# A two-layer graph convolution: layer 2's first chunks gather rows before they are normalised

## The chip, the cores and the metric

The kernel runs on one core of a Trainium2 chip. The metric is the device time of one execution in microseconds (us). The kernel before takes 2332.54 us, the median of three runs (2331.6 to 2333.5). The engines are called by their names in the profile: PE is TensorE (PEld its weight loads), DVE is VectorE, ACT is ScalarE, POOL is GpSimd, SP is SyncE, which here only issues transfers.

## What is computed

A graph of N = 6250 nodes (128 features) and E = 106250 edges, sorted by destination, goes through two attention layers with two heads of 64 columns. Between them every feature is normalised over all nodes and passed through a ReLU. The result is added to the input and each row is normalised.

```python
def conv(h, edge_attr, src, dst, Wq, bq, Wk, bk, Wv, bv, We, Ws, bs):
    q, k, v = (heads(h @ W + b) for W, b in ((Wq, bq), (Wk, bk), (Wv, bv)))
    e = heads(edge_attr @ We)
    alpha = einsum('ehc,ehc->eh', q[dst], k[src] + e) / sqrt(C)
    a = softmax of alpha over the edges of one dst
    return segment_sum((v[src] + e) * a[:, :, None], dst) + h @ Ws + bs
...
edge_attr = concatenate([cos((last_update[src] - t)[:, None] * time_w + time_b), msg])
h = conv(x, edge_attr, ...)
mu = h.mean(axis=0)
var = ((h - mu) ** 2).mean(axis=0)
h = relu((h - mu) / sqrt(var + 1e-05) * bn_g + bn_b)
out = layernorm(x + conv(h, edge_attr, ...))
```

Layer 2 needs mu and var over all nodes, so nothing of its scores can be computed before layer 1 has ended. The product k[src] is not formed: q is multiplied with the weights of k ahead of time and stored per destination node (the "tables"), so that a chunk's scores are products of raw source rows with a table.

## The kernel before

A plan at the start cuts the sorted edges into NC = 107 chunks of consecutive destination nodes, each of at most 1024 edges (T = 8 tiles of 128) and at most NN = 64 nodes. It computes the first node of each chunk (nbs) and its first edge (sls). If the plan's limits hold, `ordered` runs; otherwise `general`, which is another program for the same result.

`ordered` runs `conv(0, ...)` and `conv(1, ...)`, one loop over the chunks each, written out by hand in program order (`manual_schedule`). For chunk k:

- `fetch(k)` (L714): SP loads the edge attributes into the tile ff, the chunk's part of the table (ftab), and in layer 2 the stored time encoding (fz), the stored transposed edge attributes (into fxT, which serves as their buffer) and the residual rows (fr).
- `gather(k)` (L740): eight indirect transfers issued by GpSimd, each of 128 source rows, from xv_d in layer 1 and from h_d in layer 2.
- `turn_in` (L783): TensorE transposes the gathered rows (fpx), ScalarE copies them out of PSUM (fft). Layer 1 also transposes the edge attributes.
- `score` (L803), `lowest`, `weigh`: scores in PSUM (fps), their minimum per row on VectorE, the exponential on ScalarE (fs).
- `turn_weights` (L824), `gather_sums` (L835): weights transposed (fpt), then eight products accumulate the sums of a chunk in fpa.
- `divide`, `finish_turn`, `finish` (L841 to L897): division, multiplication with Wv and We. Layer 1 stores the chunk's columns into hT (features on partitions, nodes along the free axis), layer 2 adds the residual and collects groups of chunks (STARTS) for the row norm.

In a round k of the loop the chunks k+4 (fetch, gather), k+1 (turn_in), k (score), k-1 (sums) and k-2 (finish) are in work. Layer 1's time encoding is a sine on ScalarE, one chunk at a time for the first rounds (up to SINGLE = 24), then in pairs; the sine and the exponential are in different function tables.

The tables of a layer are made in blocks of 512 nodes (`tables`, L622): layer 1 has five products of 128x512 a block, layer 2 four, each evacuated with a bias, and the block stored with one transfer issued by ScalarE. `residual` makes res_d, x + h @ Ws + bs, in layer 2. Block 0 of layer 1 is made in the plan. The other blocks come from a generator `extra`, of which `pull` takes steps: in layer 1 six steps at round -4 and one step in each round, in layer 2 one step in each round from -4, with blocks 0 and 1 made before the loop.

Between the loops (L975 to L1046), outside of a manual order: the mean by a sum over one half of hT on VectorE and of the other half on ScalarE (L982, L983), the variance by one pass of ScalarE over hT (L988), scale and shift, and then for each of 13 blocks a ReLU with scale and shift on ScalarE (L1003), four transposes on TensorE (L1006), a copy on VectorE into one of four buffers (L1008), and a store to h_d by SP (L1011). The gathers of layer 2 read h_d and wait for all of these stores.

Of the kernel before, what the change touches and what calls it, by code (L numbers as in the profile page):

```python
# [7 lines left out]
F32 = mybir.dt.float32  # L8
I32 = mybir.dt.int32
AF = mybir.ActivationFunctionType  # L10
# [34 lines left out]
T = 8  # L45
CE = T * P
NN = P // H
NC = 107
EW = ED + 1

BITS = 8
# [4 lines left out]
HIGHEST = 2.0 ** 119  # L56

LG = 10
STARTS = (*range(0, 91, LG), 98, 102, 104, 105, 106)


@with_exitstack
# [558 lines left out]

def tables(nc, pl, c, fT, b0, work, bank):  # L622

    o = work.tile([P, GE, H, 3 - c], F32, name="fo", tag="fo")
    for i, (a, b) in enumerate(pl.mats[c]):
        pg = bank()
        nc.tensor.matmul(pg, a, fT, start=True, stop=True)  # L627
        if i == 2 * H:
            nc.scalar.activation(o[:, :, :, 2], pg[:, :, None].to_broadcast([P, GE, H]), AF.Identity, bias=b)
        elif i < H:  # L630
            nc.scalar.activation(o[:, :, i, 0], pg, AF.Identity, bias=b)
        else:
            nc.vector.scalar_tensor_tensor(
                o[:, :, i - H, 1].rearrange("p (b n) -> p b n", n=P), pg.rearrange("p (b n) -> p b n", n=P), b,
                pl.code[:, None, :].to_broadcast([P, GE // P, P]), op0=OP.add, op1=OP.add)
        if i == len(pl.mats[c]) - 1:
            nc.scalar.dma_start(pl.tab_d[c][:, b0 * GE:(b0 + 1) * GE], o)
        yield
# [22 lines left out]
def ordered(ctx: ExitStack, tc: tile.TileContext, pl, x, dst, edge_attr_64, conv2, bn_g, bn_b, out):  # L661
# [9 lines left out]
    const = ctx.enter_context(tc.tile_pool(name="fconst", bufs=1))  # L671
    dram = ctx.enter_context(tc.tile_pool(name="fdram", bufs=1, space=bass.MemoryType.DRAM))
    h_d = dram.tile([N, D], F32, name="h_d")
    res_d = dram.tile([NP, D], F32, name="res_d")

    enc_d = dram.tile([NC, P, T * TD], F32, name="enc_d")
# [12 lines left out]

    AHEAD = 4  # L690

    SINGLE = 24

    def conv(c, extra):


        cs = ExitStack()
# [42 lines left out]
        def gather(k):  # L740
            f = ch[k].f
            for t in range(T):
                nc.gpsimd.indirect_dma_start(  # L743
                    out=f[:, t, (1 if c else 0):1 + D], out_offset=None, in_=h_d if c else pl.xv_d,
                    in_offset=bass.IndirectOffsetOnAxis(ap=pl.srcs[:, t, k:k + 1], axis=0))

        shape = [P, T, TD]
# [35 lines left out]
        def turn_in(k, u):  # L783

            s = ch[k]
            if u == 0:
                s.ft = work.tile([P, CE], F32, name="fft")
                if c == 0:
                    s.et = work.tile([EC, CE], F32, name="fet")
            px = p_tr.tile([P, GE], F32, name="fpx", tag="tr")  # L790
            for t in range(4):
                nc.tensor.transpose(px[:, t * P:(t + 1) * P], s.f[:, u * 4 + t, 1:1 + D], ident)  # L792
            nc.scalar.copy(s.ft[:, u * GE:(u + 1) * GE], px)  # L793
            if c:
                return
            pe = p_tr.tile([P, GE], F32, name="fpe", tag="tr")
            for t in range(4):
                nc.tensor.transpose(pe[:EC, t * P:(t + 1) * P], s.f[:, u * 4 + t, 1 + D:], ident)
            nc.scalar.copy(s.et[:, u * GE:(u + 1) * GE], pe[:EC])  # L799
            if u:  # L800
                nc.sync.dma_start(et_d[k], s.et)
# [39 lines left out]
        def divide(k):  # L841
            s = ch[k]
            inv = small.tile([P, 1], F32, name="finv")
            nc.vector.tensor_scalar(inv, s.pa[:, D + ED:], 1e-30, None, op0=OP.max)
            nc.vector.reciprocal(inv, inv)
            s.a = small.tile([P, D + EW], F32, name="fa")
            nc.vector.tensor_scalar(s.a, s.pa, inv, None, op0=OP.mult)  # L847

        def finish_turn(k):
            s = ch[k]  # L850
# [56 lines left out]
        def pull(gen, n):  # L907
            for _ in range(n):
                next(gen, None)

        with cs, tc.manual_schedule():
            for k in range(-AHEAD, NC + 3):
# [3 lines left out]
                if on(k + AHEAD):  # L916
                    fetch(k + AHEAD)
                    gather(k + AHEAD)
                if k == -AHEAD and c == 0:
                    pull(extra, 6)  # L920
                if on(k):
                    score(k, 0)
                if on(k - 1):
# [16 lines left out]
                for j in (k + 2,) if k < SINGLE else (k + 2, k + 3) if k == SINGLE else (k + 3,):  # L940
                    if c == 0 and on(j):
                        encode(j)
                        if j < SINGLE + 3:
                            sine()
                pull(extra, 1)
                if len(args) == 3 or args and k == NC - 4:
                    sine()
                if on(k - 2):
                    finish(k - 2)
                if c and on(k):  # L950
                    nc.vector.tensor_copy(ch[k].f[:, :, 1 + D:1 + D + TD], ch[k].z)
                for _ in range(min(len(done), 2 if k > NC - 12 else 1)):
                    store(*done.pop(0))
                if on(k - 1):
                    gather_sums(k - 1)
            for _ in extra:
                pass
            for rows in done:
# [5 lines left out]
    with tc.tile_pool(name="fpw", bufs=2) as pw:  # L964
        with tc.tile_pool(name="ftp", bufs=3, space=bass.MemoryType.PSUM) as mp, tc.manual_schedule():
            turn_features(nc, pl, mp, N)
        def rest():
            for b0 in range(1, NT):
                yield from tables(nc, pl, 0, xT[:, b0 * GE:(b0 + 1) * GE], b0, pw, lambda: pl.bank())
                if b0 == 2:  # L970
                    yield from load_others(nc, pl, const, conv2, bn_g, bn_b)
            yield from matrices(nc, pl, 1, const, lambda: pl.bank()[:, :P])

        conv(0, rest())
    nc.gpsimd.memset(hT[:, N:], 0.0)  # L975


    with tc.tile_pool(name="fbn1", bufs=1) as one, tc.tile_pool(name="fbnw", bufs=2) as pw:
        neg = one.tile([P, 2], F32, name="fmu")
        half = N // 2  # L980
        scr = pl.xT
        nc.vector.tensor_reduce(neg[:, 0:1], hT[:, :half], AX.X, OP.add)  # L982
        nc.scalar.activation(scr[:, half:N], hT[:, half:N], AF.Copy, accum_out=neg[:, 1:])  # L983
        mu = one.tile([P, 1], F32, name="fmu1")
        nc.vector.tensor_add(mu, neg[:, 0:1], neg[:, 1:])
        nc.vector.tensor_scalar(mu, mu, -1.0 / N, None, op0=OP.mult)
        var = one.tile([P, 1], F32, name="fbvar")
        nc.scalar.activation(scr[:, :N], hT[:, :N], AF.Square, bias=mu, accum_out=var)  # L988
        nc.vector.tensor_scalar(var, var, 1.0 / N, EPS, op0=OP.mult, op1=OP.add)
        nc.scalar.activation(var, var, AF.Sqrt)  # L990
        scale = one.tile([P, 1], F32, name="fscale")
        nc.vector.reciprocal(scale, var)
        nc.vector.tensor_mul(scale, scale, pl.bng)
        shift = one.tile([P, 1], F32, name="fshift")
        nc.vector.tensor_mul(shift, scale, mu)
        nc.vector.tensor_add(shift, shift, pl.bnb)
        NB = -(-N // P)
        with tc.tile_pool(name="fbnh", bufs=4) as hp, \
                tc.tile_pool(name="fbnp", bufs=2, space=bass.MemoryType.PSUM) as pps:
            for b0 in range(0, NB, 4):  # L1000
                n = min(4, NB - b0)
                cs_ = slice(b0 * P, b0 * P + GE)
                nc.scalar.activation(hT[:, cs_], hT[:, cs_], AF.Relu, bias=shift, scale=scale)  # L1003
                pt = pps.tile([P, 4, P], F32, name="fpt")
                for i in range(n):
                    nc.tensor.transpose(pt[:, i], hT[:, (b0 + i) * P:(b0 + i + 1) * P], ident)  # L1006
                hr = hp.tile([P, 4, P], F32, name="fhr")
                nc.vector.tensor_copy(hr[:, :n], pt[:, :n])  # L1008
                full = min(n, (N - b0 * P) // P)
                if full:  # L1010
                    nc.sync.dma_start(h_d[b0 * P:(b0 + full) * P, :].rearrange("(b p) d -> p b d", p=P), hr[:, :full])  # L1011
                if full < n:
                    left = N - (b0 + full) * P
                    nc.sync.dma_start(h_d[(b0 + full) * P:N, :], hr[:left, full])

        def residual(b0):

# [21 lines left out]
            next(res, None)  # L1039
            yield  # L1040

        with tc.tile_pool(name="fpp2", bufs=1, space=bass.MemoryType.PSUM) as pp:
            pl.bank = lambda: pp.tile([P, GE], F32, name="fpg")
            for b0 in range(2):
                for _ in block(b0):
                    pass  # L1046

        def rest():
            for b0 in range(2, NT):
                yield from block(b0)  # L1050

        conv(1, rest())
    nc.sync.dma_start(out[N - NN:N, :], tail_d[NN:2 * NN, :])


@with_exitstack
def tile_gnn_resnorm(ctx: ExitStack, tc: tile.TileContext, x, src, dst, edge_attr_64, edge_weight, node_vec,
# [13 lines left out]
    with tc.tile_pool(name="plan", bufs=1) as pl, tc.tile_pool(name="planw", bufs=2) as mw, \  # L1071
# [5 lines left out]
                                                  ap=[[step, r1 - r0], [1, P]]))  # L1077
        NP = got.NP = -(-(N + NN) // GE) * GE
        got.hT = keep.tile([P, NP], F32, name="fhT")
        got.rest = keep.tile([P, 1 + D], F32, name="fxrest")  # L1080
        got.raw, got.web, got.ws, got.mats = {}, {}, {}, ([], [])

# [22 lines left out]
        nc.vector.tensor_scalar(ident, jpp, 0.0, None, op0=OP.is_equal)  # L1105
        nxt = pl.tile([P, NC], F32, name="nxt")
        nc.vector.tensor_scalar(nxt, jpp[:, :NC], 1.0, None, op0=OP.is_equal)
        ones = pl.tile([P, P], F32, name="pones")
        nc.vector.memset(ones, 1.0)
        ends = pl.tile([1, 2, NC + 1], F32, name="ends")  # L1110
        nc.vector.memset(ends[:, 0, NC:], float(N))
# [154 lines left out]
```

## Time and profile before

One execution was recorded with a profile. It took 2840.8 us, longer than a run without recording (2332.54); its span is 2838.6 us and the mean granted TensorE clock 0.94 of full speed.

| what | value |
|---|---|
| median of the runs | 2332.54 us |
| the profiled execution, its span | 2840.8, 2838.6 us |
| PE, POOL, DVE, ACT busy | 2380.1, 1637.7, 1246.3, 1236.5 us |
| gathers of layer 1 and of layer 2 (856 each) | 822.3 and 810.9 us, 961 and 947 ns each |
| moved by the transfers | 396.58 MB, mean 140 GB/s |

A busy share is an average over the start, two loops, the stretch between them and the end. The stretch between the loops is seen best in order of time. In lines of the timeline the columns are start, duration (both us), engine, source line, operation, result and operands, number of instructions, and in brackets the idle time of the engine ahead of it with what ended it. "issue" is a wait that the profile shows no cause of, "remote" one for a semaphore whose sender isn't known. A float32 product shows up as two records.

### The profile page before, as it was taken

The page shows a single profiled execution, that of the slowest core. Times are in us where ns is not written, and L with a number is a line of the kernel's source. Part 1 is how long each engine was busy: PE and PEld are TensorE (multiplying, and loading weights), DVE is VectorE, ACT ScalarE, POOL GpSimd, SP SyncE. Part 2 cuts the span into 40 slices and gives each one's busy share as a digit, 9 for nine tenths or more (in the row PEclk, how much of TensorE's full clock was granted, in tenths as well). Part 3 has the DMA queues.
Part 4 walks back from the last instruction along what each step waited for, and adds up shares of the span by engine and source line. Part 5 has one row for each costly group of instructions (what it writes and reads, how often), then busy time and mean ns, then how long its engine had stood idle before and what let it go on. Part 6 is the DMA issues. An engine that isn't in the chain of part 4 may idle for free.

```text
span 2838.6 us, 39250 instructions
## 1 busy us (share of the span) xinstructions
PE 2380.1 (84%) x11637; PEld 1759.9 (62%) x11637; DVE 1246.3 (44%) x3735; ACT 1236.5 (44%) x1950; POOL 1637.7 (58%) x1733
## 2 busy tenths in 40 slices
PE   5589988888988888888965989988998888888887
PEld 3366766666776776666742666656666665666665
DVE  3446665555665566565621333333333222222223
ACT  2356664455554455544541333333433333333334
POOL 4356665655665666666415666666666666666661
PEclk7799999999999999999976999999999999999998
DMA  6345554555554445454425555655555454444541
GB/s 198 116 117 155 157 151 144 146 144 166 157 155 127 124 135 137 134 136 136 124 75 165 154 151 155 170 147 156 156 152 151 133 138 127 133 128 131 136 127 46
DMA packets 428354, 396.58 MB, mean 140 GB/s; under 512 B 282064, under 2 KB 371940, under 8 KB 424804
## 3 DMA queue, kind: packets, MB, share of 16 engines
q1 hardware_dynamic: 354406, 238.66, 30.3%
q0 software_dynamic: 55168, 114.12, 15.7%
q10 hardware_dynamic: 18558, 41.20, 3.9%
q8 instruction: 95, 1.56, 0.2%
q14 instruction: 127, 1.04, 0.1%
HBM read 279.72 MB, written 110.59 MB: 138 GB/s over the span
## 4 chain that ended last, share of the span: by engine, by line
PE 34%; issue 6%; another core or an unknown queue 3%; DVE 3%; DMA 2%; POOL 2%; ACT 1%; SPq 1%; DVEq 0%; ACTq 0%; POOLq 0%
PE fpa L839 11%; PE fps L809 6%; PE fps L810 5%; PE fppt L832 4%; PE fpx L792 3%; POOL ff L743 2%; PE fpo L875 1%; PE fpg L627 1%; DMA fr<-res_d 1%; PE fpo L853 1%; DMA ff<-h_d,fsrcs 1%; PE fpo L876 1%; DVE fa L847 1%; PE fpo L854 0%
## 5 line engine op out<-in xcount | busy, mean ns | idle before, releaser
L743 POOL DMA_INDIRECT ff<-xv_d,fsrcs x856 | 822.3, 961 | 568.3 <-issue 224.4
L743 POOL DMA_INDIRECT ff<-h_d,fsrcs x856 | 810.9, 947 | 517.9 <-issue 249.9
L839 PE MATMUL fpa<-ff,fpt 128*128 128x225 f32 x3424 | 714.6, 362 | 0.8 <-issue 0.8
L839 PEld LDWEIGHTS fpa<-ff,fpt 128*128 128x128 f32 x3424 | 645.9, 194 | 14.6 <-issue 0.9
L809 PE MATMUL fps<-fft,ftab 128*128 128x512 f32 x856 | 464.7, 622 | 74.2 <-issue 33.0
L793 ACT COPY fft<-fpx 128x512 f32<-128x512 f32 x428 | 250.2, 585 | 545.7 <-PE fpx L792 202.3
L832 PEld LDWEIGHTS fppt<-fident,fs 128*128 128x128 f32 x1712 | 208.6, 144 | 201.8 <-issue 194.9
L832 PE MATMUL fppt<-fident,fs 128*128 128x128 f32 x1712 | 253.8, 279 | 79.0 <-issue 77.0
L833 ACT COPY fpt<-fppt 128x512 f32<-128x512 f32 x428 | 227.6, 581 | 117.8 <-PE fppt L832 50.0
L822 ACT ACTIVATE fs<-fps,fm 128x1024 f32<-128x1024 f32 x214 | 238.7, 1115 | 66.1 <-issue 27.6
L815 DVE TENSOR_REDUCE flow<-fps 128x1 f32<-128x1024 f32 x214 | 260.0, 1215 | 12.5 <-PE fps L810 12.5
L792 PE MATMUL fpx<-fident,ff 128*128 128x128 f32 x1712 | 254.1, 284 | 12.1 <-DVE fbits L726 12.1
L891 ACT ACTIVATE fsq<-fy 64x128 f32<-64x128 f32 x107 | 33.1, 310 | 503.7 <-DVE fy L889 286.4
L887 DVE SCALAR_TENSOR_TENSOR fres<-fpo,fr 64x128 f32<-64x128 f32 x107 | 30.2, 282 | 501.5 <-PE fppt L832 211.0
L810 PE MATMUL fps<-fxT,ftab 112*128 112x512 f32 x428 | 231.3, 618 | 7.3 <-issue 6.4
L809 PEld LDWEIGHTS fps<-fft,ftab 128*128 128x128 f32 x856 | 171.7, 230 | 104.1 <-issue 56.1
L810 PE MATMUL fps<-fet,ftab 112*128 112x512 f32 x428 | 224.3, 605 | 0.8 <-issue 0.8
L792 PEld LDWEIGHTS fpx<-fident,ff 128*128 128x128 f32 x1712 | 209.8, 147 | 17.1 <-DVE fbits L726 13.7
L799 ACT COPY fet<-fpe 112x512 f32<-112x512 f32 x214 | 126.3, 590 | 198.1 <-PE fppt L832 56.0
L853 PEld LDWEIGHTS fpo<-fident,fa 128*128 128x128 f32 x214 | 30.5, 142 | 286.8 <-issue 184.9
L856 DVE COPY fat<-fpo 128x256 f32<-128x256 f32 x214 | 90.9, 425 | 247.9 <-PE fpo L854 102.5
L853 PE MATMUL fpo<-fident,fa 128*128 128x128 f32 x214 | 64.0, 299 | 157.1 <-DVE fa L847 95.3
(198 smaller groups left out, 2540.7 us busy)
## 6 DMA issues: line engine op xcount, KB each, us to landing
ff<-in_edge_attr SPq DMA_DIRECT2D x214, 256.0 KB
et_d<-fet SPq DMA_DIRECT2D x107, 448.0 KB
fxT<-et_d SPq DMA_DIRECT2D x107, 448.0 KB
ftab<-tab_d SPq DMA_DIRECT2D x107, 192.0 KB
tab_d<-fo ACTq DMA_DIRECT2D x13, 1536.0 KB
ff<-xv_d,fsrcs POOLq DMA_INDIRECT x856
enc_d<-fzs SPq DMA_DIRECT2D x107, 128.0 KB
ff<-h_d,fsrcs POOLq DMA_INDIRECT x856
```

The costliest lines, as they stand in the source:

```text
L743: nc.gpsimd.indirect_dma_start(out=f[:, t, (1 if c else 0):1 + D], out_offset=None, in_=h_d if c else pl.xv_d, in_offset=bass.IndirectOffs ...
L792: nc.tensor.transpose(px[:, t * P:(t + 1) * P], s.f[:, u * 4 + t, 1:1 + D], ident)
L793: nc.scalar.copy(s.ft[:, u * GE:(u + 1) * GE], px)
L799: nc.scalar.copy(s.et[:, u * GE:(u + 1) * GE], pe[:EC])
L809: nc.tensor.matmul(s.ps[:, w], s.tab[:, :, 0], s.ft[:, w], start=True, stop=False)
L810: nc.tensor.matmul(s.ps[:, w], s.tab[:EC, :, 1], s.et[:, w], start=False, stop=True)
L815: nc.vector.tensor_reduce(low, s.ps, AX.X, OP.min)
L822: nc.scalar.activation(s.s, s.ps, AF.Exp, bias=s.bias, scale=-1.0)
L832: nc.tensor.transpose(pp[:, t * P:(t + 1) * P], s.s[:, at:at + P], ident)
L833: nc.scalar.copy(s.pt[:, u * GE:(u + 1) * GE], pp)
L839: nc.tensor.matmul(s.pa, s.pt[:, t * P:(t + 1) * P], s.f[:, t, 1:1 + D + EW], start=t == 0, stop=t == T - 1)
L853: nc.tensor.transpose(s.po[:, 0], s.a[:, :D], ident)
```

## The change

NC becomes 106, with STARTS to match; SINGLE becomes 16.

In layer 1 no step of `extra` is taken before round 0; two are taken in rounds 0 to 3 and above 80, one in the others. The tiles fo get one buffer. After the tables and matrices the generator takes layer 1's results block by block, once the rounds have passed that can still write into the block: `pass_rows` transposes the raw block of hT, copies it, takes its moments with bn_stats, and SP stores the raw rows into h_d.

After the loop bn_aggr joins the moments; scale and shift follow. Before layer 2's loop only block 0 gets its ReLU, its table and its residual, on three PSUM banks instead of one, and scale and shift are spread over partitions (`spread`). In round -4 of layer 2, after the fetch and gather of chunk 0, `first_blocks` applies the ReLU to the other blocks of hT, transposes all 13 blocks and stores them into a second array, hn_d, by transfers that ScalarE issues.

Chunks 0 to 2 (RAW = 3) gather raw rows from h_d. Their transposed rows get scale, shift and ReLU when ScalarE takes them out of PSUM, and the rows themselves by three operations of VectorE (`normalise`). All later chunks gather from hn_d. Block 1 of layer 2's table is made in rounds 0 to 2.

```diff
-NC = 107
+NC = 106
...
-    o = work.tile([P, GE, H, 3 - c], F32, name="fo", tag="fo")
+    o = work.tile([P, GE, H, 3 - c], F32, name="fo", tag="fo", bufs=1)
...
-    SINGLE = 24
-
-    def conv(c, extra):
+    SINGLE = 16
+
+    RAW = 3
+
+    def conv(c, extra, first_blocks=None):
...
-                    out=f[:, t, (1 if c else 0):1 + D], out_offset=None, in_=h_d if c else pl.xv_d,
+                    out=f[:, t, (1 if c else 0):1 + D], out_offset=None, in_=(h_d if k < RAW else hn_d) if c else pl.xv_d,
...
-            nc.scalar.copy(s.ft[:, u * GE:(u + 1) * GE], px)
+            if c and k < RAW:
+                nc.scalar.activation(s.ft[:, u * GE:(u + 1) * GE], px, AF.Relu, bias=pl.shift, scale=pl.scale)
+            else:
+                nc.scalar.copy(s.ft[:, u * GE:(u + 1) * GE], px)
...
+        def normalise(k):
+            rows = ch[k].f[:, :, 1:1 + D]
+            for i, op in enumerate((OP.mult, OP.add)):
+                nc.vector.tensor_tensor(rows, rows, pl.spread[:, None, i].to_broadcast([P, T, D]), op)
+            nc.vector.tensor_scalar(rows, rows, 0.0, None, op0=OP.max)
...
-                if k == -AHEAD and c == 0:
-                    pull(extra, 6)
+                if k == -AHEAD and c:
+                    first_blocks()
...
-                pull(extra, 1)
+                if k >= 0:
+                    at_round[0] = k
+                    pull(extra, 2 if k < 4 or k > 80 else 1)
...
                 if c and on(k):
+                    if k < RAW:
+                        normalise(k)
...
+        def pass_rows(b0):
...
+            rows = turned_rows(b0)
+            nc.vector.bn_stats(stats[:, b0], hT[:, r0:r0 + n])
+            yield
+            put_rows(nc.sync, h_d, b0, rows)
+            yield
+
+        def turned_rows(b0):
...
+                nc.tensor.transpose(pt[:, i], hT[:, r0 + i * P:r0 + (i + 1) * P], ident)
+            rows = pw.tile([P, GE // P, P], F32, name="fhr", bufs=3)
+            nc.vector.tensor_copy(rows[:, :n], pt[:, :n])
+            return rows
...
         def rest():
+            others = load_others(nc, pl, const, conv2, bn_g, bn_b)
             for b0 in range(1, NT):
                 yield from tables(nc, pl, 0, xT[:, b0 * GE:(b0 + 1) * GE], b0, pw, lambda: pl.bank())
-                if b0 == 2:
-                    yield from load_others(nc, pl, const, conv2, bn_g, bn_b)
+
+                for _ in range(2):
+                    next(others, None)
+                    yield
             yield from matrices(nc, pl, 1, const, lambda: pl.bank()[:, :P])
+            for b0 in range(-(-N // GE)):
+
+                while at_round[0] < 3 + max(k for k in range(NC) if first(k)[0] < (b0 + 1) * GE):
+                    yield
+                yield from pass_rows(b0)
...
-        nc.vector.tensor_reduce(neg[:, 0:1], hT[:, :half], AX.X, OP.add)
-        nc.scalar.activation(scr[:, half:N], hT[:, half:N], AF.Copy, accum_out=neg[:, 1:])
...
-        nc.scalar.activation(scr[:, :N], hT[:, :N], AF.Square, bias=mu, accum_out=var)
...
+        nc.vector.bn_aggr(moments, stats)
...
-                nc.scalar.activation(hT[:, cs_], hT[:, cs_], AF.Relu, bias=shift, scale=scale)
...
-                    nc.tensor.transpose(pt[:, i], hT[:, (b0 + i) * P:(b0 + i + 1) * P], ident)
...
-                    nc.sync.dma_start(h_d[b0 * P:(b0 + full) * P, :].rearrange("(b p) d -> p b d", p=P), hr[:, :full])
...
+        def first_blocks():
+
+            for b0 in range(1, NT):
+                relu(b0)
+            for b0 in range(-(-N // GE)):
+                put_rows(nc.scalar, hn_d, b0, turned_rows(b0))
...
-        with tc.tile_pool(name="fpp2", bufs=1, space=bass.MemoryType.PSUM) as pp:
+        with tc.tile_pool(name="fpp2", bufs=3, space=bass.MemoryType.PSUM) as pp, tc.manual_schedule():
             pl.bank = lambda: pp.tile([P, GE], F32, name="fpg")
-            for b0 in range(2):
-                for _ in block(b0):
-                    pass
+            relu(0)
+            for _ in block(0):
+                pass
...
         def rest():
-            for b0 in range(2, NT):
+            for b0 in range(1, NT):
                 yield from block(b0)
-
-        conv(1, rest())
+                yield
+                yield
+
+        conv(1, rest(), first_blocks)
```

`put_rows(eng, to, b0, rows)` issues, on the engine eng, the one or two transfers that store a block's rows.

## The prediction, made before the changed kernel ran

> **What bounds the kernel now.** I read the page first (shares, then the groups), then TensorE's order of time inside a loop, then the stretch between the layers on all engines, then the same stretch in slices of 10 us.
>
> ```profile
> PE 2380.1 (84%) x11637; PEld 1759.9 (62%) x11637; DVE 1246.3 (44%) x3735; ACT 1236.5 (44%) x1950; POOL 1637.7 (58%) x1733
> ...
> L743 POOL DMA_INDIRECT ff<-h_d,fsrcs x856 | 810.9, 947 | 517.9 <-issue 249.9
> L839 PE MATMUL fpa<-ff,fpt 128*128 128x225 f32 x3424 | 714.6, 362 | 0.8 <-issue 0.8
> ```
>
> TensorE is the busiest engine. GpSimd comes second: one gather takes 0.95 us and the next begins 0.30 us later, so the eight gathers of a chunk need 8 x 1.25 = 10.0 us. In the order of time, layer 2's early rounds look like this:
>
> ```profile
> 1560.33 3.21 PE L839 MATMUL fpa<-ff,fpt 128*128 128x225 f32 x16
> 1568.78 1.02 PE L627 MATMUL fpg<-fhT,fm 128*128 128x512 f32 x2
> 1570.36 3.31 PE L839 MATMUL fpa<-ff,fpt 128*128 128x225 f32 x16
> 1580.50 3.31 PE L839 MATMUL fpa<-ff,fpt 128*128 128x225 f32 x16
> ```
>
> A round takes 10.1 us and TensorE has no gap in it; 0.86 of that is one product of the table work (L627), so 9.25 without. Layer 1's undisturbed rounds (1406.6 to 1426.5) take 9.83 us. Over whole layers the first fpa to the last gives more: (1441.3 - 129.1)/106 = 12.38 us a chunk in layer 1, (2818.8 - 1560.3)/106 = 11.87 in layer 2. The profiled execution took 2840.8 us (span 2838.6), the median of the runs is 2332.5, a factor 0.821; 12.1 x 0.821 = 9.95 us. So without the recording a chunk costs close to its TensorE work, and also close to GpSimd's 10.0 us. Either way a chunk is 9.9 us.
>
> The stretch between the layers:
>
> ```profile
> 1453.09 5.50 ACT L988 ACTIVATE fxT<-fhT,fmu 128x6250 f32<-128x6250 f32 x1 [0.47 <-DVE fmu L986]
> 1463.81 11.58 SPq L1011 DMA_DIRECT2D h_d<-fhr  x12
> 1475.31 2.08 PE L627 MATMUL fpg<-fhT,fm 128*128 128x512 f32 x2 [1.99 <-DVE fhr L1008]
> 1480.20 0.95 POOL L743 DMA_INDIRECT ff<-h_d,fsrcs  x1 [30.13 <-issue]
> 1488.54 0.36 ACTq L637 DMA_DIRECT2D tab_d<-fo  x1
> 1504.61 0.35 ACTq L637 DMA_DIRECT2D tab_d<-fo  x1
> 1512.09 1.04 PE L792 MATMUL fpx<-fident,ff 128*128 128x128 f32 x8
> 1531.72 0.59 ACT L793 COPY fft<-fpx 128x512 f32<-128x512 f32 x1 [14.95 <-issue]
> 1532.36 2.08 PE L809 MATMUL fps<-fft,ftab 128*128 128x512 f32 x2 [14.40 <-issue]
> 1543.65 2.08 PE L809 MATMUL fps<-fft,ftab 128*128 128x512 f32 x2 [7.85 <-ACT fft L793]
> ```
>
> Call t = 0 the end of layer 1's last fpa (1444.5). Then: last hT store landed t = 5, mean and variance over all of hT to t = 16, thirteen relus, transposes and row stores to t = 31 (landed 34.4), first gather t = 35.7, two table blocks to t = 60, transposes of chunk 0 at t = 67.6, first score at t = 87.9. The first fpa of layer 2 starts 119 us after layer 1's last.
>
> ```profile
> 1500.00:1510.00 10.00, 6.80 (x14) 3.46 (x14) 3.63 (x5) 0.00 (x0) 7.56 (x9) 0.50 0.83 255
> 1520.00:1530.00 10.00, 0.00 (x0) 0.00 (x0) 1.14 (x2) 0.00 (x0) 7.56 (x9) 0.50 0.50 137
> ```
>
> Columns: PE, PEld, DVE, ACT, POOL busy, granted clock, DMA share, GB/s. From 1513 to 1547 all but GpSimd nearly stand still, with "issue" as the reason, while 48 gathers go out back to back; the start of layer 1 shows the same (from 49 to 105). I take most of these stalls to belong to the recording: if all of them were in the plain runs too, 90 us of start and stalls would leave less per chunk than TensorE's own work. So in a plain run the first score stands near t = 70.
>
> **What the Trainium skill says.** "DMA: Bandwidth & Descriptors", section Issuing engines are not separate DMA queues: transfers issued from different engines share the same 16 DMA engines and interleave; another issuer saves only issue time. So storing by ScalarE buys no bandwidth, it only keeps SP free. The trace of before has h_d at 3.2 MB in the 15 us from 1463.8 to 1478.8, 213 GB/s, through SP. "TensorE: Matmul & The Clock Gate", section What's actually happening: after an idle window the clock falls to half. The trace agrees: granted 0.50 in the stretch, 2.08 us for a product that takes 1.02 in the loop. "ScalarE: Activation LUTs", section What ACT_TABLE_LOAD costs: an activation with pointer operands costs some hundred ns more than a copy; here L1003 takes 0.80 us, L793's copy 0.59.
>
> **The change part by part.**
>
> *One chunk fewer per layer.* In the profile 12.38 + 11.87 = 24.2 us; in a plain run 2 x 9.9 = 20. A chunk's work is fixed (1024 slots), so no other chunk grows. Counting the inputs' dst, the fullest of 106 chunks has 1023 edges and 63 nodes (limits 1024 and 64), so the fast path is still taken.
>
> *Between the layers.* Statistics: the two passes (2.8 + 5.5 us) go; bn_stats per block goes into layer 1's last rounds. After t = 0: fat copy, then the copy and bn_stats of block 11 ahead of fres on VectorE (0.69 + about 0.6, so +1.3), hT landed t = 6.5; last block's transpose, copy, bn_stats, bn_aggr and six small operations of 0.16 to 0.2: shift at t = 9.5. First relu 0.8: t = 10.3. One table block instead of two, on three banks instead of one: four products at half clock, 4 x 2.08: t = 18.6; VectorE 1.1: table stored from t = 20. Residual 2.1, two adds, res_d at t = 23; the relus queued on ScalarE end at t = 26. Then first_blocks: TensorE has 49 transposes ahead of chunk 0's, VectorE 13 copies through three buffers, ScalarE 13 stores ahead of chunk 0's evacuation. So chunk 0 waits for the last row store to be *issued*. In before a buffer came back 2.5 to 4.3 us after its copy (L1008's waits for "DMA h_d<-fhr", with four buffers). With 0.7 of copy and 3.3 of return for three buffers: 1.33 us a block, 13 blocks 17 us; with the raw gathers and fetches beside it I take 5 us and so 21: t = 47. Chunk 0's own data are there by then (raw h_d landed t = 11, gathers to t = 23, table and fetches by t = 35). First score t = 47 against 70 in a plain run: -23 (ends -45 and 0). In the profile against 87.9, keeping half of the 28 us of stalls: about -38.
>
> *The gathers.* Chunks 0 to 2 gather from h_d at t = 11 to 41. Chunk 3's wait for hn_d, t = 49, then 10 + 2 us: t = 61; TensorE asks for it in round 2, near t = 47 + 24. Queued behind it on GpSimd are all later gathers, each 10 us against TensorE's 9.8: 10 us of slack. If GpSimd is the true bound, the gain is gather 3 at 49 instead of 35.7 + 30 = 65.7: -16.
>
> *Work put into the loops, where nothing covers it on TensorE.* 49 transposes of raw rows at 0.11 us: +5.3. Layer 2's block 1: four products of 0.86 and one of 0.87: +4.3. Nine table products of layer 1 that stood before round 0: +7.7, against a start that reaches chunk 0 earlier (gather 0 ends near 50, those products and their evacuations run 63 to 104 in the profile): I take -8, ends -20 and 0, so net 0.
>
> *Edits at nothing.* 13 copies and bn_stats (nearest row 0.69 us each, 17 us together) lie on VectorE, 42 of 71 us busy there; uncovered they would cost 17. normalise on three chunks: three operations of 1024 columns, 0.6 to 1.2 us each, 2.9 a chunk, on VectorE at a third busy, due a round later. Relu in place of the copy for three chunks: 6 x 0.2 us. fo with one buffer: a block's first write comes three rounds (30 us) after the previous store, in the doubled first rounds one (about 12 us, for 1.5 MB): 0 to 5 once. SINGLE 24 to 16: eight rounds with one less pair of table loads (2.6 us on ScalarE); the profile's early single rounds take 12.0 us, the paired ones after them 12 to 13, so 0, ends -8 and +3. SP: 13 more row stores in layer 1 behind VectorE's copy, 0.4 us each, SP waits anyway.
>
> Sum in a plain run: -20 - 23 + 9.6 = -33, 2299. In the profile's own time: -24.2 - 38 + 9.6 - 5 = -58, 2783, times 0.821 = 2285. I take 2291.
>
> **Rivals.**
> A, the forecast: 2280 to 2305. Chance 0.45.
> B, the stall goes as well: the 48 gathers now come as 24 and 24, and if the stalls of 28 us are in plain runs too, 2332 - 20 - 50 + 5 = 2267. For it: the trace shows the stall only in gather bursts. Against: the 0.821. Chance 0.22.
> C, only the chunks count: the row stores hold chunk 0 to t = 65, or gathers bound and gain little: 2332 - 20 - 5 + 9.6 = 2317. Chance 0.2.
> D, slower: ScalarE's and VectorE's queues stand on the return of the three row buffers. In before a 32 KB load issued in this stretch (fr<-res_d, 1494.9) was 28 us under way. At a return of r us, chunk 0 waits 25 + 13/3 x (r + 0.7); the gain of 33 is used up at r = 12, and at r = 20 the total is 2332 - 20 + 45 + 9.6 = 2367. Against it: stores came back in 2.5 to 4.3 us. Chance 0.08.
> E, the change does not do what it says (106 chunks fail the plan's test, general path): far above 3000; excluded by the count unless I miscounted, 0.01. The remaining 0.04 lies within 0.2% of 2332.5, which is about what a measurement can tell.
>
> **How the numbers follow.** Faster than 2327.9: 0.87, same 0.04, slower 0.09. The range takes A, most of B and C: 2260 to 2321.
>
> **What would show it.** In the changed trace: last fpa of layer 1 to first of layer 2 near 80 us (119 before); hn_d stores spanning 15 to 25 us and ended just ahead of chunk 0's transposes; L749's gather of chunk 3 after the last store; 106 fpa groups per layer with the same spacing. Wrong: VectorE's copies waiting over 10 us each on "DMA hn_d<-fhr", or TensorE idle at chunk 3.

## The result, and the profile after

The changed kernel takes 2301.03 us (median of four, 2299.42 to 2308.59) against 2332.07 for the kernel before: the ratio is 0.9876, 95% interval 0.9862 to 0.989, and the gain 31 us. The forecast was 2291, its range 2260 to 2321.

The profiled execution of the kernel before that the prediction was read from (2840.8 us) was an outlier: the same program recorded again took 2330.41 us (span 2328.2), so that recording is used below (`before_again`). Five of the experiments were measured under conditions in which every run of every kernel took a fifth to a quarter longer, for a reason that no trace names, and their times are compared only with the runs of the kernel before beside them.

The page of the changed kernel (its recorded execution was the longest of the four, 2308.59 us, span 2306.8):

```profile
PE 2214.9 (96%) x11586; PEld 1711.8 (74%) x11586; DVE 1240.1 (54%) x3738; ACT 1195.2 (52%) x1919; POOL 1629.7 (71%) x1717
...
L748 POOL DMA_INDIRECT ff<-hn_d,fsrcs x824 | 782.6, 950 | 261.6 <-issue 216.4
L847 PE MATMUL fpa<-ff,fpt 128*128 128x225 f32 x3392 | 694.9, 357 | 0.0
```

TensorE is busy for 96% of the span, as in `before_again`, which reads as "TensorE is the bound". The rest of this text shows why that reading misleads in layer 2. Rounds in the order of time, TensorE alone:

```profile
1703.90 1.02 PE L627 MATMUL fpg<-fhT,fm 128*128 128x512 f32 x2
1705.48 3.31 PE L847 MATMUL fpa<-ff,fpt 128*128 128x225 f32 x16
1714.05 1.02 PE L627 MATMUL fpg<-fhT,fm 128*128 128x512 f32 x2
1715.62 3.31 PE L847 MATMUL fpa<-ff,fpt 128*128 128x225 f32 x16
```

A round with a table product (L627) takes 10.1 us (1715.62 - 1705.48), as before. The stretch between the layers, all engines, t = 0 at the end of layer 1's last fpa (1186.36):

```profile
1207.18 22.98 ACTq L1012 DMA_DIRECT2D hn_d<-fhr  x12
...
1227.80 0.69 DVE L1004 COPY fhr<-fpg 128x512 f32<-128x512 f32 x1 [4.26 <-DMA hn_d<-fhr]
...
1230.92 1.45 ACT L799 ACTIVATE fft<-fpx,fshift,fscale 128x512 f32<-128x512 f32 x2 [23.30 <-DMA hn_d<-fhr]
1231.75 2.08 PE L817 MATMUL fps<-fft,ftab 128*128 128x512 f32 x2 [2.09 <-ACT fft L799]
...
1236.96 0.94 POOL L748 DMA_INDIRECT ff<-hn_d,fsrcs  x1 [10.71 <-DMA fr<-res_d]
...
1249.26 3.20 PE L847 MATMUL fpa<-ff,fpt 128*128 128x225 f32 x16
```

ScalarE needs 23 us for twelve stores, in which VectorE's copies wait up to 4.26 us for one of three buffers to come back; only then does ScalarE take chunk 0 out of PSUM, and the first score stands at t = 45.4. GpSimd has gathered three raw chunks by then and stood still for 10.71 us; its first gather of normalised rows, chunk 3's, is at t = 50.6. (The bracket names a load, fr<-res_d, but that gather reads hn_d, so it also needs all stores of hn_d to have landed, and the last is issued after 1230.16.) The same places in the kernel before, recorded again (t = 0 at 1182.77):

```profile
1202.07 10.12 SPq L1011 DMA_DIRECT2D h_d<-fhr  x12
...
1217.52 0.95 POOL L743 DMA_INDIRECT ff<-h_d,fsrcs  x1 [29.18 <-ACT fo L631]
```

SP issued its twelve stores in 10.1 us with no gather and no fetch beside them, the first gather (chunk 0's) was at t = 34.8, and the first score, at 1249.67, at t = 66.9.

What GpSimd waits for from there to the end (engine, line, what it waited for: us in total, times, longest us), in the changed kernel, 1250 to 2290 us:

```profile
POOL ff L748 <- issue: 213.7, 701, 0.3
POOL ff L748 <- DMA ff<-hn_d,fsrcs: 7.9, 26, 0.3
```

and in the kernel before, the same window:

```profile
POOL ff L743 <- issue: 223.5, 733, 0.3
POOL ff L743 <- PE fpa L839: 3.7, 12, 0.3
```

These are the two largest entries of each list; in neither list is a wait longer than 0.3 us, the ordinary distance between two gathers. From its first gather of normalised rows on GpSimd never stops in layer 2, in either kernel: eight gathers of 1.25 us make its chunk 10.0 us long. TensorE, over the same window of the changed kernel, does stop:

```profile
PE fpx L797 <- DMA ff<-hn_d,fsrcs: 11.2, 24, 1.1
```

These 24 short waits come late: up to about chunk 77 TensorE works off what was gathered ahead (rounds of 9.3 and 10.1 us), from there on its rounds are about 10.0 us although the table work is over, because it has caught up with GpSimd (a round without table work takes it 9.3 where nothing holds it). POOL at 71% busy hides this, since its 0.3 us between gathers do not count as busy.

### The profile page after: what moved, and what is told of

The parts are those of the page before. It is cut to its first block, busy times and chain, and to the rows that moved or that the text cites. A ratio compares the mean times of both kernels' runs of the same rounds, so it can differ in the third digit from the quotient of the medians.

```text
span 2306.8 us, 39033 instructions
## 1 busy us (share of the span) xinstructions
PE 2214.9 (96%) x11586; PEld 1711.8 (74%) x11586; DVE 1240.1 (54%) x3738; ACT 1195.2 (52%) x1919; POOL 1629.7 (71%) x1717
## 5 line engine op out<-in xcount | busy, mean ns | idle before, releaser
L748 POOL DMA_INDIRECT ff<-hn_d,fsrcs x824 | 782.6, 950 | 261.6 <-issue 216.4
L847 PE MATMUL fpa<-ff,fpt 128*128 128x225 f32 x3392 | 694.9, 357 | 0.0
L847 PEld LDWEIGHTS fpa<-ff,fpt 128*128 128x128 f32 x3392 | 628.9, 190 | 11.8 <-issue 1.0
L817 PE MATMUL fps<-fft,ftab 128*128 128x512 f32 x848 | 443.5, 605 | 3.7 <-ACT fft L799 2.1
L840 PE MATMUL fppt<-fident,fs 128*128 128x128 f32 x1696 | 220.1, 272 | 0.0
L818 PEld LDWEIGHTS fps<-fet,ftab 112*128 112x128 f32 x424 | 106.3, 251 | 75.8 <-issue 58.2
L818 PEld LDWEIGHTS fps<-fxT,ftab 112*128 112x128 f32 x424 | 84.1, 198 | 99.9 <-issue 99.2
L772 DVE SCALAR_TENSOR_TENSOR farg<-fturns,farg 128x256 f32<-128x256 f32 x318 | 135.4, 426 | 10.9
L852 DVE TENSOR_SCALAR finv<-fpa 128x1 f32<-128x1 f32 x212 | 32.5, 153 | 196.1 <-DMA ff<-hn_d,fsrcs 88.7
L806 PE MATMUL fpe<-fident,ff 128*112 128x128 f32 x848 | 130.1, 277 | 2.8 <-DVE ff L784 1.5
```

The costliest lines, as they stand in the source:

```text
L748: nc.gpsimd.indirect_dma_start(out=f[:, t, (1 if c else 0):1 + D], out_offset=None, in_=(h_d if k < RAW else hn_d) if c else pl.xv_d, in_o ...
L772: nc.vector.scalar_tensor_tensor(arg, turn, -part, arg, op0=OP.mult, op1=OP.add)
L817: nc.tensor.matmul(s.ps[:, w], s.tab[:, :, 0], s.ft[:, w], start=True, stop=False)
L818: nc.tensor.matmul(s.ps[:, w], s.tab[:EC, :, 1], s.et[:, w], start=False, stop=True)
L840: nc.tensor.transpose(pp[:, t * P:(t + 1) * P], s.s[:, at:at + P], ident)
L847: nc.tensor.matmul(s.pa, s.pt[:, t * P:(t + 1) * P], s.f[:, t, 1:1 + D + EW], start=t == 0, stop=t == T - 1)
```

## The experiments

Twelve runs follow. The first repeats the kernel before; the next three ask what the parts of the change are worth.

**before_again.** The kernel before, unchanged, recorded once more.

> The kernel before, once more under the recording. Theory (the long profile of before, 2840.8 us, was an execution held up by its recording): the new span lies near 2330, rounds of layer 1 and 2 take 9.8 and 9.3 us plus 0.86 for a table product, and the stretch from layer 1's last fpa to layer 2's first is near 90 us, with the first score about 70 us after the end of layer 1. Rival (the stalls of 1513 to 1547 belong to the kernel): the stretch is again near 119 us.

Measured: 2330.41 us, span 2328.2, clock 0.98. This recording did not lengthen the execution: it lies within the unrecorded runs (2329.11 to 2335.28). The stalls from 1513 to 1547 us that the prediction put down to the recording did not come back (the first score is at t = 66.9, not 87.9), so recording alone does not make them; what made that one execution slow isn't known.

**after_107.** The changed kernel with one chunk more.

```diff
-NC = 106
+NC = 107
-STARTS = (*range(0, 91, LG), 97, 101, 103, 104, 105)
+STARTS = (*range(0, 91, LG), 98, 102, 104, 105, 106)
```

> The changed kernel with 107 chunks and the STARTS of before. Theory (a chunk is worth 9.9 us a layer): 2301 + 20 = 2321. Rival (the chunk is hidden in one layer because another engine sets its end): 2311. A second rival, that most of the gain is the stretch between the layers: 2306.

Measured: 2324.2 us (2323.3 to 2328.56), ratio 0.9967 (0.9954 to 0.9979): 23.2 us above the changed kernel.

**before_106.** The kernel before with the same edit the other way round, nothing else.

> The kernel before with 106 chunks and the STARTS of the change, nothing else. Theory: 2332 - 20 = 2312. If it is 2322, a chunk is worth half of what I took; if 2301, the rest of the change did nothing.

Measured: 2308.56 us (2308.37 to 2310.83), ratio 0.9902 (0.9886 to 0.9919): 23.6 us below the kernel before. The two agree: the chunk count is worth 23.5 us, three quarters of the whole gain, and all the rest of the change nets 7.5 us (2308.56 to 2301.03). after_107 has that rest alone against the kernel before: 8.0 us, by the interval of its ratio 5 to 11.

**raw_0.** The changed kernel with no raw chunk: all gathers read hn_d. The block stores stand ahead of chunk 0's fetch and gather, since that gather waits for them.

```diff
-    RAW = 3
+    RAW = 0
...
+                if k == -AHEAD and c:
+                    first_blocks()
                 if on(k + AHEAD):
                     fetch(k + AHEAD)
                     gather(k + AHEAD)
-                if k == -AHEAD and c:
-                    first_blocks()
```

> The changed kernel with RAW = 0: the row stores of first_blocks come ahead of the first gather, and all chunks gather normalised rows. Theory (GpSimd's gathers set the end of layer 2): the gather of chunk 3 moves from 50 us after layer 1's end to about 46 + 30 = 76, so +26, 2327. Rival (TensorE's rounds set it, and only chunk 0's lateness counts: first score at 60 instead of 45): +15, 2316. Second rival (raw rows were not needed, other waits cover it): 2301.

Measured: 2331.85 us (2329.84 to 2338.08), ratio 1.0004 (0.9995 to 1.0013): 30.8 us above the changed kernel. The raw chunks are worth 31 us, more than any theory gave them. Its trace shows where they are lost:

```profile
1202.73 20.64 ACTq L1012 DMA_DIRECT2D hn_d<-fhr  x12
1231.29 0.95 POOL L748 DMA_INDIRECT ff<-hn_d,fsrcs  x1 [91.93 <-DMA ff<-in_edge_attr]
```

The first gather is at t = 49.3 (layer 1 ended at 1181.95), 14.6 us later than in before_106, although the first score, at 1242.9, is 8 us *earlier* after layer 1's end than there. Layer 2 follows the gather: its last fpa starts 1131.5 us after layer 1's end, against 1116.9, which is again 14.6 later. Beside the changed kernel, where it starts 1103.5 us after layer 1's end, raw_0 loses 28.0 us in layer 2.

That gives a rule that the later runs could be held against. In each recording take the first gather of normalised rows, chunk j's, and the start of layer 2's last fpa:

| kernel | layer 1 ends | first score, t | first normalised gather, t | gather to last fpa | span |
|---|---|---|---|---|---|
| before_again (107 chunks) | 1182.8 | 66.9 | chunk 0, 34.8 | 1091.9, 107 chunks left | 2328.2 |
| before_106 | 1173.4 | 69.2 | chunk 0, 34.7 | 1082.2, 106 left | 2306.8 |
| raw_0 | 1182.0 | 61.0 | chunk 0, 49.3 | 1082.2, 106 left | 2329.9 |
| changed kernel | 1186.4 | 45.4 | chunk 3, 50.6 | 1052.9, 103 left | 2306.8 |
| after_107 | 1194.7 | 46.1 | chunk 3, 51.7 | 1063.9, 104 left | 2326.8 |
| one_step_b | 1174.5 | 44.6 | chunk 3, 50.5 | 1053.0, 103 left | 2294.5 |
| raw4_onestep | 1174.3 | 46.2 | chunk 4, 52.0 | 1043.2, 102 left | 2288.8 |
| all_three_b | 1173.9 | 38.4 | chunk 4, 50.2 | 1043.0, 102 left | 2284.7 |

With the same number of chunks left, the time from the gather to the end is the same within 0.3 us, whatever the first score does; each chunk more costs about 10 us. Counted from the first score to the last fpa, the six kernels of 106 chunks range from 1047.6 to 1070.5. No run made a gather cheaper or shortened a chunk's row of gathers, which would be the most direct test.

**raw_4, one_step, more_buffers, old_moments.** Three edits that should each gain some 10 us, and one that takes the new moments back. They are four of the five runs under the conditions in which every kernel took longer.

```diff
-    RAW = 3
+    RAW = 4
```

> Four chunks of layer 2 gather raw rows instead of three, so GpSimd's next gather after the normalised rows are stored is chunk 4's and not chunk 3's; one more chunk is normalised in the rows by VectorE (3.2 us) in the round of chunk 3. If GpSimd's row of gathers (8 x 1.25 = 10.0 us a chunk, begun again at 1236.96 in the changed kernel after an idle 10.71 us) sets the end of layer 2, the stop of 10.7 us is filled with chunk 3's gathers: 2291 us, 10 below the changed kernel, and TensorE waits less for gathered rows late in layer 2. If TensorE's own rounds set the end, nothing changes but one more normalise: 2301 to 2304 us.

```diff
-                    pull(extra, 2 if k < 4 or k > 80 else 1)
+                    pull(extra, 2 if k < 4 or k > 87 else 1)
```

> The steps of the work beside layer 1 are taken one a round up to round 87, instead of two a round from round 81 on. If the two steps of matrices in one round are what makes the two rounds of 14.9 us (TensorE waits for the copy, its clock-like pace falls and a score takes 5.06 us instead of 3.21), these rounds fall to 10.5 us and layer 1 ends about 9 us earlier: 2292 us. If those rounds only use time that is lost later in the layer anyway, 2301 us as before.

```diff
...
-                put_rows(nc.scalar, hn_d, b0, turned_rows(b0))
+                rows = None
+                if b0 < 8 or b0 > 10:
+                    i = b0 if b0 < 8 else b0 - 11
+                    if i % 2 == 0:
+                        pair = work.tile([P, CE], F32, name=("fs", "fpt")[i // 2 % 2])
+                    rows = pair[:, i % 2 * GE:(i % 2 + 1) * GE].rearrange("p (b d) -> p b d", d=P)
+                put_rows(nc.scalar, hn_d, b0, turned_rows(b0, rows))
```

> The copies of the normalised rows are staged in the work tiles of the loop as well (8 more halves beside the three buffers), so that no copy waits for a store to land. If the three buffers hold the stores back (copies of the changed kernel wait up to 4.26 us on hn_d<-fhr), the twelve stores are done about 10 us earlier, the first score starts at 35 us after layer 1's last sum instead of 45.4, GpSimd's idle 10.71 us ahead of chunk 3's gather goes, and the time is 2291 to 2293 us. If the stores are bound by what the DMA engines move (3 MB beside raw gathers), the last store lands where it did and the time is 2301 us.

```diff
-            nc.vector.bn_stats(stats[:, b0], hT[:, r0:r0 + n])
...
-        nc.vector.bn_aggr(moments, stats)
+        nc.vector.tensor_reduce(neg[:, 0:1], hT[:, :half], AX.X, OP.add)
+        nc.scalar.activation(scr[:, half:N], hT[:, half:N], AF.Copy, accum_out=neg[:, 1:])
...
+        nc.scalar.activation(scr[:, :N], hT[:, :N], AF.Square, bias=mu, accum_out=std)
```

> The moments come from the two passes over hT between the layers, as in the kernel before, in place of one bn_stats a block inside layer 1's loop and one bn_aggr; the rest of the change stays. The passes stand on the path between the layers: half a sum and half a copy beside each other and one square pass over all of it, some 3 and 5.5 us, with three small VectorE steps more; bn_aggr (0.51 us) goes. Eleven bn_stats of 0.68 us leave VectorE in layer 1, which is not its bound there. The theory that moments by blocks take about 9 us out of the stretch expects 2309 to 2312 us; if layer 1 gains what the stretch loses, 2301 to 2304.

Measured, against 2785.54 us for the kernel before beside them: raw_4 2739.05, ratio 0.9845 (0.9807 to 0.9884); one_step 2738.88, 0.9827 (0.9795 to 0.9859); more_buffers 2737.85, 0.9823 (0.9792 to 0.9855); old_moments 2749.85, 0.9862 (0.9816 to 0.9908). The four intervals overlap and the changed kernel was not run beside them, so the times separate nothing. One reading holds all the same, since it concerns a few instructions only. In old_moments:

```profile
1402.68 2.81 ACT L1037 ACTIVATE fxT<-fhT 128x3125 f32<-128x3125 f32 x1 [10.28 <-DMA fhT<-fres]
...
1406.05 5.50 ACT L1042 ACTIVATE fxT<-fhT,fmu 128x6250 f32<-128x6250 f32 x1 [0.48 <-DVE fmu L1040]
...
1414.05 0.81 ACT L1080 ACTIVATE fhT<-fhT,fshift,fscale 128x512 f32<-128x512 f32 x1 [0.89 <-DVE fshift L1050]
```

Layer 1's last fpa ended at 1396.51, so the first ReLU is at t = 17.5. In raw_4, under the same conditions with moments by blocks, it is at t = 8.3 (in one_step and more_buffers 8.4):

```profile
1399.84 0.51 DVE L1035 BATCH_NORM_AGGREGATE fmom<-fstats 128x2 f32<-128x78 f32 x1
...
1401.58 0.81 ACT L1074 ACTIVATE fhT<-fhT,fshift,fscale 128x512 f32<-128x512 f32 x1 [0.81 <-DVE fshift L1044]
```

(last fpa ended at 1393.25). Moments by blocks bring the first ReLU 9.2 us forward, as expected; whether this reaches the end of the kernel was not measured.

**all_three.** raw_4, one_step and more_buffers together.

> The three edits of raw_4, one_step and more_buffers together. If each acts where it was thought to (GpSimd's idle time ahead of the first gather of normalised rows 10.7 us, the two rounds of 14.9 us some 9 us, the late first score partly the same 10 us as GpSimd's), the changed kernel would gain 9 from layer 1 and about 12 from the start of layer 2: 2280 us, which is 0.978 of the kernel before, where the changed kernel has 0.9876. If layer 1's rounds and the stores' landing were not what held them, 2301 us, 0.987.

Measured: 2787.95 us against 2891.61, ratio 0.9611 (0.9557 to 0.9666), again under such conditions. It gains more there than any of its parts did, but the kernel before had itself moved from 2785 to 2892, so this says little of the parts. The same kernel was measured once more, with the kernel before back at 2331.

> The kernel of all_three once more, on a chip where the kernel before takes 2332 us again, so that its time can be put beside the changed kernel's 2301. The theory of the three causes (gathers that stop for 10.7 us, row buffers that hold the stores back, two matrices steps a round) expects 2280 us; if layer 1's rounds and the stores' landing were not what held them, 2301. Where the kernel before is again above 2700 us, the ratio is to be within 0.956 to 0.967 as in all_three.

Measured: 2285.17 us (2284.68 to 2286.95) against 2331.23, ratio 0.9804 (0.979 to 0.9817). This is the best version found: 16 us below the changed kernel, 46 below the kernel before. From its first raw gather (t = 10.0) to its last gather GpSimd has no wait over 0.31 us. Two kernels share these 16 us out.

**one_step_b.**

> The kernel of one_step again where the kernel before takes 2332 us. all_three_b took 2285.2, 16 below the changed kernel; its layer 1 lasted 12.5 us less between first and last sum than in the profile of the changed kernel, its start of layer 2 7.2 less. If two matrices steps in a round are what cost layer 1 the two rounds of 14.9 us, this kernel alone takes 2291 us (ratio 0.9825); if layer 1's gain comes from something else in all_three_b, 2301 (0.9870).

Measured: 2296.27 us (2292.81 to 2299.6), ratio 0.9843 (0.983 to 0.9857): 4.8 us by the medians, 7.7 by the ratios (0.0033 x 2332). It lies between the two theories' values. The recorded executions of the changed kernel and of one_step_b are 10.3 us apart in layer 1, from its first sum to its last (1104.2 and 1093.9), but raw_0, whose layer 1 is the changed kernel's own program, took 1100.2, so some 6 us are the edit's and the rest varies from run to run. The local effect is clear. In the changed kernel, TensorE alone:

```profile
925.70 3.21 PE L847 MATMUL fpa<-ff,fpt 128*128 128x225 f32 x16
...
938.28 0.79 PE L595 MATMUL fpg<-ftr,ftr 64*128 64x128 f32 x2 [2.50 <-ACT fft L801]
940.61 5.06 PE L847 MATMUL fpa<-ff,fpt 128*128 128x225 f32 x16
...
955.50 4.45 PE L847 MATMUL fpa<-ff,fpt 128*128 128x225 f32 x16
```

In one_step_b:

```profile
931.19 3.21 PE L847 MATMUL fpa<-ff,fpt 128*128 128x225 f32 x16
940.67 0.49 PE L595 MATMUL fpg<-ftr,ftr 64*128 64x128 f32 x2
941.75 3.21 PE L847 MATMUL fpa<-ff,fpt 128*128 128x225 f32 x16
951.23 0.48 PE L595 MATMUL fpg<-ftr,ftr 64*128 64x128 f32 x2
952.31 3.21 PE L847 MATMUL fpa<-ff,fpt 128*128 128x225 f32 x16
```

With two steps in a round the second small product (L595) waits 2.50 us for a copy on ScalarE, and the eight sums (L847) after it take 5.06 us instead of 3.21. The two rounds are 14.9 us long (925.70, 940.61, 955.50); with one step a round is 10.6 (931.19, 941.75, 952.31). The granted clock in that stretch, by slices (columns: stretch, its length, busy time and instructions of PE, PEld, DVE, ACT, POOL, then clock, DMA share, GB/s), in the changed kernel:

```profile
940.00:955.00 15.00, 13.82 (x64) 11.30 (x64) 6.04 (x18) 5.05 (x10) 6.92 (x8) 0.84 0.45 112
```

and in one_step_b:

```profile
940.00:955.00 15.00, 15.00 (x88) 12.94 (x87) 11.19 (x36) 10.53 (x17) 11.35 (x12) 1.00 0.57 153
```

Such a round is 4.3 us longer than one with a single step: 2.5 are the wait itself, and 1.85 of the rest are the sums at the lower clock. raw_0 and after_107, which also take two steps, show the same wait of 2.49 us and sums of 4.9 and 5.3 us after it.

**raw4_onestep.**

> raw_4 and one_step without the further row buffers, so that its difference to one_step_b is the fourth raw chunk alone and its difference to all_three_b the buffers alone. GpSimd as the bound of layer 2: the idle time ahead of the first gather of normalised rows goes, 10 us more than one_step_b: 2281 to 2283 us, and the buffers of all_three_b bring nothing. TensorE as the bound, with a first score that waits for ScalarE's twelve stores: the fourth raw chunk brings 0 to 2 us, 2289 to 2291, and the buffers of all_three_b the rest, 5 to 7.

Measured: 2289.93 us (2288.3 to 2293.11), ratio 0.9817 (0.9804 to 0.9831), 6.3 us below one_step_b beside it. The time itself lies in the second theory's window, but only because one_step_b came out at 2296 and not 2291; of the differences that the theories are about, the fourth raw chunk brought 6.3 (10 against 0 to 2 expected) and the buffers of all_three_b 4.8 (0 against 5 to 7). By the times alone that is open; the traces decide. In raw4_onestep:

```profile
1220.52 2.07 PE L817 MATMUL fps<-fft,ftab 128*128 128x512 f32 x2 [4.19 <-ACT fft L799]
...
1226.24 0.94 POOL L748 DMA_INDIRECT ff<-hn_d,fsrcs  x1 [1.84 <-issue]
```

The first score is 1.6 us later than in one_step_b (t = 46.2 after 44.6), the first normalised gather is chunk 4's at t = 52.0 where chunk 4 would have had 50.5 + 10 = 60.5, and GpSimd's idle time ahead of it is 1.84 us instead of 10.85. From layer 1's end to the last fpa it takes 1095.2 us instead of 1103.5: 8.3 less, as GpSimd's 8.5 says and not as the later score does. Against it all_three_b, with the further buffers:

```profile
1212.26 2.08 PE L817 MATMUL fps<-fft,ftab 128*128 128x512 f32 x2 [11.29 <-ACT fft L799]
...
1224.08 0.94 POOL L748 DMA_INDIRECT ff<-hn_d,fsrcs  x1 [0.30 <-issue]
```

The score comes 7.8 us earlier (t = 38.4), the gather 1.8 us, and layer 2 ends 2.0 us earlier after layer 1. The times differ by 4.8 us, the ratios by 3.0; of the 4.1 between the two spans 2.0 are in layer 2, 0.4 ahead of it, and 1.6 behind the last fpa, where recordings of all kernels differ by as much (16.5 to 19.3 us). So the three row buffers did hold up the first score, as expected, but the first score is not what counts; and with GpSimd's idle time down to 1.84 us there was little left for more buffers to fill. The stores themselves gained 6 us of 23 only. Beside raw gathers and fetches they stay slower than SP's 10.1 us, and the 16 DMA engines then show no idle time (share 1.09, 317 GB/s, from 1194.0 to 1211.5; 0.88 and 254 GB/s during SP's stores in before_again, 1202.0 to 1212.7). That goes with what the Trainium skill says ("DMA: Bandwidth & Descriptors", Issuing engines are not separate DMA queues): transfers run on the same 16 DMA engines whichever engine issued them, so another issuer brings no bandwidth of its own. No run here changed the issuer alone, so its share isn't separated.

## Why the prediction was nearly right

The forecast of faster held, and the sum in a plain run (2299) came within 2 us of the median; the value put forward, 2291, is 10 us too low. That the sum fits so well is in part luck: the start of layer 2 gained 13 to 14 us and not 23, and this was made up for by a chunk that is worth 3.5 us more than foretold and by work in layer 2's loop that cost nothing measurable. By its own steps:

- *One chunk fewer, 20.* Right in kind, 23.5 in size. The recordings show 9.4 us by layer 1's end (1182.8 to 1173.4), 9.7 in layer 2 after the first gather, and 2.3 behind the last fpa, which varies by that much without a change of the count.
- *Between the layers, -23, from a first score at 47 instead of 70.* The times are right: 45.4 and 66.9. First ReLU foretold at 9.5, measured 8.3; row stores to end at 47, the last issued at 44. The last fpa of layer 1 and the first of layer 2 start 66.1 us apart, 83.4 in before_again. What failed is the choice of the first score as the thing that sets layer 2's end. The step named the other value in one sentence, gather 3 "at 49 instead of 35.7 + 30 = 65.7: -16", if GpSimd is the true bound. It is: the gather came at 50.6 instead of 34.8 + 30, so -14.2. The "10 us of slack" against TensorE's 9.8 us a chunk was a misreading: by its own figures TensorE gains 0.2 us a chunk on GpSimd, 20 us over 100 chunks, which is more than the slack, and its rounds without a table product are 9.3.
- *Work in the loops, +9.6.* Layer 2's share (+4.3) fell on TensorE while GpSimd set the end, so it cost nothing measurable. In layer 1 the recorded executions of before_106 and of the changed kernel differ by 10.1 us. Above a bare round of 9.83, the table rounds cost nearly the same in both (46.0 before, 46.7 after), so the nine products weighed next to nothing; the matrices took 12.2 instead of 4.7, the two rounds in which the sine goes over to pairs 10.1 instead of 4.3, what follows (without the last two rounds) 5.0 instead of 8.8. Two matrices steps a round, at a fallen clock, were not in the sum, and the switch of the sine at round 16 was put at 0. The switch varies between recordings (10.1 here, 7.3 in one_step_b, 6.9 in raw_0), and between 10.1 and 6.9 the difference goes with the clock: TensorE waits 3.05 us in the second of these rounds here and 2.52 in raw_0, and the granted clock in the 10 us from 260 is 0.66 here and 1.00 there. Why it fell in one and not in the other is not settled.
- *The start, -8 against the products.* It did not come: the first fpa starts at 82.2 us, in before_106 at 79.3.
- *The profile's own time, 2783 x 0.821 = 2285, which pulled 2299 down to 2291.* Wrong. The stalls halved in it came back neither in the second recording nor in the program's ordinary runs, and the -5 in its sum stands for no named part. The plain sum alone was the better forecast by 8 us.
- *Rivals.* The time fell in A's window. B (the stalls go as well, 2267) fell with before_again. D's mechanism is real in small: three buffers, copies waiting for up to 4.26 us, and more buffers brought the first score 7.8 us forward; the price was 2 to 5 us. C (gathers bound, 2317) had the right bound and gave it 5 us where it was worth 14.2.

The recorded executions of before_106 and of the changed kernel are equally long (span 2306.8 each): layer 2 gained 13.3 us after layer 1's end, start and layer 1 gave 13.0 back. The medians differ by 7.5, since the recorded one of the changed kernel was its longest; in which rounds its other runs save that isn't known.

## What to carry to other kernels

Ask which engine never waits, not which is busiest: GpSimd at 71% with 0.3 us between its gathers ran without a stop from its first gather of normalised rows to its last, and set the end of layer 2 while TensorE stood at 96% over the whole span. For such an engine only the moment it starts counts, and what fills its stops: here one more raw chunk was worth more (8.3 us of layer 2) than a first score 7.8 us earlier (2.0). Spread small steps that wait for another engine over rounds instead of doubling them up, and look at the clock after the wait as well as at the wait.

## What the runs showed of the hardware

The same kernel, the one before, took 2331 to 2332 us in most measurements and 2785 and 2892 us in two others, in every run of them. In the longer ones each engine's instructions are about as long (a gather 946 ns in one_step against 950 in the changed kernel, the sums of L847 360 against 357), with more time between them, whose cause the traces don't name. It is not shown to belong to a chip: the record numbers the chip of the 2892 us and that of 2331 us within the hour after it both as 1. The first recording of the kernel before looks like one of these: there GpSimd waited up to 23.4 us in layer 2's loop, in the second recording never over 0.3. A profile taken under such conditions misplaces the bound.

A wait of TensorE of 2 to 3 us in a dense loop can lower the clock for what follows, but did not each time: after 2.50 us sixteen records of L847 took 5.06 us instead of 3.21, with a clock of 0.84 over 15 us; after 2.52 us in raw_0, at the switch of the sine, the clock stayed at 1.00.

Moments by blocks cost VectorE 0.68 us for 512 columns and 0.51 us to join, against 2.81 and 5.50 us of passes on ScalarE.
